# Mean over graph edges with sorted key windows: one-operand target compares, TensorE in program order, and key fetches for two slots at once

## The chip, the cores and the metric

The kernel runs on one core of one Trainium2 chip. The metric is device microseconds of one execution. A core has TensorE (PE, with its weight loads as PEld), VectorE (DVE), ScalarE (ACT), GpSimd (POOL) and SyncE (SP); each runs its own list of instructions in order, and semaphores tie the lists together.

## What is computed

One layer of a graph network: 100,000 nodes with 64 features, 3,300,000 edges sorted by target node, a self edge for every node among them.

```
h = maximum(_layernorm(x, axis=-1), 0.0)
local, nbr = h[dst], h[src]
y = concatenate([local, nbr - local], axis=-1) @ W.T + b
s, cnt = segment_sum(y, dst), segment_sum(1, dst)
x = x + where(cnt > 0, s / max(cnt, 1), 0)
```

As y is linear, each target needs only the sum of its sources' rows of h and their count. Finding and summing the source rows of 3.3 million edges is the work.

## The kernel before

`h3` holds each node's row of h as three bf16 parts (192 columns) and a column of ones. The edges go two ways.

**Gathered chunks** (`chunks`): the last 354 chunks of 3584 edges. For each group of 128 edges POOL gathers 128 rows of `h3` with an indirect DMA (L388, into `nb`, a ring of 42), DVE builds a one-hot matrix of the targets (`hot`, L331), and PE multiplies the two into `ps` (L399), 21 gathers behind the issue. After 28 of them DVE sums the three parts (L404) and POOL adds the result to `acc` in DRAM (L357, L362), due 56 gathers later.

**Windows**: the first 2.03 million edges, as 256 windows of 7936 edges. `sort_windows` sorts each window's keys by source on DVE and ACT and writes them to `ksort`; it then counts where each cell of 256 source nodes begins in each window (L596 and after) and writes these places to `at` (L627 to L636). `fill_slots` fetches for every block of 512 source nodes ("slot", 196 of them and 4 for self edges) the first 32 keys of each cell from `ksort`, 4 fetches a slot (L716, POOL, into `kf`), and makes of them source numbers (`sr_d`) and target numbers (`dt_d`, through PE transposes L740 and ACT copies L742). Keys beyond 32 in a cell are found by `find_beyond`: up to 64 per window, 128 fetches (L692 into `kx`), and then shifts on DVE (L698).

`passes` runs over 64 sets of four windows. It holds the rows of 40 slots in SBUF (`tab`, loaded at L759) and takes one step per slot and set. In a step PE picks the rows of the keys by a one-hot of the sources (L829, 4 matmuls of 128 rows, into `gp`), ACT copies them to `gs` (L831), and PE puts them to their targets by a one-hot of the targets (L838, 16 matmuls of 32 rows, into `total`). DVE makes the one-hots for 5 steps at a time, double-buffered: `gh` by one-operand compares (L808), `dh` by `one_hot`, a compare of two operands with 512 columns per step (L331). After 40 steps `total` goes to SBUF (L863, L865) and is summed (L868). The loop handles two steps, a pair, per turn.

**Stages and order.** Sort: as the sort advances, `gathers(ns)` issues one gather per 1270 ns of estimated time. Pass 0 (slots 0 to 39, 1280 pairs): `fill` and `rest` (the generators of `fill_slots` and `find_beyond`) move on every 20 pairs, after the first 16 parts of `fill` (8 groups of 5 slots) that come ahead of it; gathers go along at about 0.8 a pair, and what is left of the first 90 chunks is drained after the pass. Passes 1 to 3 are one loop body, each with 66 chunks spread evenly over its 1280 pairs; pass 4, with the self edges and the spilled keys, is two halves of 32 sets with 33 chunks each. In these halves POOL also fetches two sets of spilled rows per four windows (L794) and adds the windows' sums (L880). A scheduler orders each engine's list from the dependencies; only what `behind`, `number` or `last` name is tied to the order of the code.

## Time and profile before

| | |
|---|---|
| median of 3 runs | 17037.5 us (17037.39 to 17084.01) |
| the profiled execution, its span | 17007.46 us, 17005.8 us |
| busy: PE, DVE, ACT, POOL | 73%, 72%, 43%, 72% |
| mean granted TensorE clock | 0.838 |
| gathers `nb` | 9912, mean 1019 ns on POOL |
| `dh` compares | 12800, mean 419 ns |
| `gh` compares | 10240, mean 393 ns |
| key fetches `kf` | 784, mean 1006 ns |

A group's row reads: line, engine, operation, output and inputs, shape, count; then busy us and mean ns of one; then the engine's idle time just ahead of these instructions and what ended it. Mean durations hold the tail of an instruction, in which the next of its engine has begun; a run of the same instruction in the timeline (x5) gives their distance. A busy PE is not a PE at its peak.

### The profile page before, as it was taken

The numbers are of one execution on the slowest core, as the hardware profiler recorded it, in microseconds if no ns is written. First come the engines' busy times: TensorE is split into PE (matmuls) and PEld (weight loads), VectorE is DVE, ScalarE is ACT, GpSimd is POOL, SyncE is SP. The second block draws the span as 40 slices with busy tenths as digits, with TensorE's granted clock in tenths as the row PEclk, the third lists the DMA queues.
The fourth block names the chain that finished last, engine by engine and source line by source line (L and its number), as shares of the span: only waits on it lengthen the run. The fifth ranks groups of instructions, "written<-read, shape, count | busy, mean of one in ns | idle before, by whom it ended". The sixth has DMA issues, their size and how long they took to land. (4 is left out here: it accounts for less than half of the span.)

```text
span 17005.8 us, 639895 instructions
## 1 busy us (share of the span) xinstructions
PE 12381.4 (73%) x266812; PEld 9784.7 (58%) x266812; DVE 12270.0 (72%) x31051; ACT 7284.1 (43%) x15555; POOL 12313.7 (72%) x11723
## 2 busy tenths in 40 slices
PE   6111111559999799999699999699999698858775
PEld 5011000447777577777577777477777576647664
DVE  6999982558878687777587777587777576647663
ACT  5244480335555344444354444254444343324331
POOL 4777777665675477777677777767777778767885
PEclk7555555779999899999799999799999798879887
DMA  7322222324454455555455555455555565556556
GB/s 293 70 39 40 49 49 58 86 73 115 120 121 120 112 128 123 124 124 122 112 127 123 124 124 123 110 128 124 122 124 123 112 125 112 113 100 121 112 111 250
DMA packets 1672971, 1949.85 MB, mean 115 GB/s; under 512 B 1065318, under 2 KB 1078766, under 8 KB 1665070
## 3 DMA queue, kind: packets, MB, share of 16 engines
q1 hardware_dynamic: 1194800, 1341.60, 27.4%
q0 software_dynamic: 471200, 541.36, 20.4%
q8 instruction: 2090, 34.24, 0.8%
q10 hardware_dynamic: 4032, 25.69, 0.4%
q14 instruction: 849, 6.96, 0.1%
HBM read 1652.22 MB, written 255.28 MB: 112 GB/s over the span
## 5 line engine op out<-in xcount | busy, mean ns | idle before, releaser
L388 POOL DMA_INDIRECT nb<-h,si x9912 | 10098.9, 1019 | 3811.3 <-issue 2714.6
L831 ACT CAST gs<-gp 128x386 bf16<-128x386 f32 x12800 | 5591.9, 485 | 7358.8 <-PE gp L829 6820.4
L331 DVE TENSOR_TENSOR dh<-dt,upto 128x512 bf16<-128x512 int16 x12800 | 4575.9, 419 | 1979.7 <-PE total L838 1697.2
L838 PE MATMUL total<-gs,dh 32*128 32x193 bf16 x200704 | 5542.2, 251 | 304.8 <-DVE dh L331 288.3
L829 PE MATMUL gp<-tab,gh 128*128 128x193 bf16 x50176 | 5509.6, 253 | 129.8 <-ACT gs L831 83.6
L838 PEld LDWEIGHTS <-dh 32*128 32x128 bf16 x200704 | 4125.9, 96 | 1490.7 <-issue 1099.5
L829 PEld LDWEIGHTS <-gh 128*128 128x128 bf16 x51200 | 4404.5, 100 | 1000.1 <-issue 861.6
L399 PE MATMUL ps<-nb,hot 128*128 128x193 bf16 x9912 | 2106.6, 278 | 3659.3 <-DMA nb<-h,si 2151.3
L808 DVE TENSOR_SCALAR gh<-srs,who_f 128x768 bf16<-128x768 int16 (+1 forms) x10240 | 3415.0, 393 | 643.5 <-PE gp L829 638.5
L399 PEld LDWEIGHTS <-hot 128*128 128x128 bf16 x9912 | 896.7, 105 | 4107.8 <-issue 2294.4
L331 DVE TENSOR_TENSOR hot<-near,upto 128x512 bf16<-128x512 int16 (+1 forms) x2832 | 925.6, 382 | 397.4 <-PE ps L399 393.0
L460 ACT COPY tmp<-keys 128x1536 f32<-128x1536 f32 (+26 forms) x525 | 647.7, 1244 | 1043.3 <-DVE keys L462 880.0
L716 POOL DMA_INDIRECT kf<-ksort,at x784 | 788.5, 1006 | 238.9 <-issue 228.9
L461 DVE TENSOR_TENSOR keys<-tmp,keys 128x1536 f32<-128x1536 f32 (+26 forms) x525 | 746.8, 1457 | 68.4 <-ACT tmp L460 67.2
L462 DVE TENSOR_TENSOR keys<-tmp,keys 128x1536 f32<-128x1536 f32 (+26 forms) x525 | 748.3, 1454 | 1.1
L868 DVE TENSOR_REDUCE wsums<-whole 128x512 f32<-128x1536 f32 x320 | 613.2, 1916 | 3.7 <-issue 2.1
L404 DVE TENSOR_REDUCE sums<-ps 128x64 f32<-128x192 f32 x354 | 123.6, 349 | 535.6 <-PE ps L399 532.4
L880 POOL DMA_DIRECT2D acc<-wsums x256 | 345.1, 1348 | 105.2 <-DMA acc<-wsums 91.0
L865 DVE COPY whole<-total 128x386 f32<-128x386 f32 x640 | 325.6, 550 | 52.2 <-ACT whole L863 52.2
L536 ACT ACTIVATE junk<-keys,bound 128x543 bf16<-128x543 f32 x450 | 337.4, 750 | 16.9 <-DVE keys L462 3.6
L863 ACT COPY whole<-total 128x386 f32<-128x386 f32 x640 | 276.4, 484 | 124.8 <-PE total L838 120.8
L362 POOL DMA_DIRECT2D acc<-sums x264 | 272.7, 1033 | 42.7 <-DMA acc<-wsums 17.4
(163 smaller groups left out, 4233.2 us busy)
## 6 DMA issues: line engine op xcount, KB each, us to landing
srs<-sr_d SPq DMA_DIRECT2D x2560, 320.0 KB
nb<-h,si POOLq DMA_INDIRECT x9912
part_d<-wsums SPq DMA_DIRECT2D x256, 260.0 KB
prev<-part_d SPq DMA_DIRECT2D x256, 260.0 KB
tab<-h SPq DMA_DIRECT2D x46, 970.0 KB
dt<-dt_d SPq DMA_DIRECT2D x2560, 10.0 KB
h<-parts SPq DMA_DIRECT2D x28, 1358.0 KB
dt_d<-dt SPq DMA_DIRECT2D x40, 640.0 KB
```

Source lines behind the costliest of these rows:

```text
L331: nc.vector.tensor_tensor(out.rearrange("p k (a d) -> p k a d", d=D), numbers[:, :, None].to_broadcast(shape), upto[:shape[0], :n].rearran ...
L388: last[POOL] = nc.gpsimd.indirect_dma_start(out=nbs[e // JN][:, e % JN], out_offset=None, in_=h3, in_offset=bass.IndirectOffsetOnAxis(ap=o ...
L399: nc.tensor.matmul(ps[:, :CE], lhsT=hots_of[d // JH][:, d % JH], rhs=nbs[d // JN][:, d % JN, :CE], start=jd == 0, stop=jd == J - 1)
L460: last[ACT] = nc.scalar.copy(tmp, lo)
L461: nc.vector.tensor_tensor(lo, tmp, hi, ALU.min)
L462: last[DVE] = nc.vector.tensor_tensor(hi, tmp, hi, ALU.max)
L716: last[POOL] = nc.gpsimd.indirect_dma_start(out=kf[:, c, r * KS:r * KS + KS], out_offset=None, in_=ksort, in_offset=bass.IndirectOffsetOnA ...
L808: nc.vector.tensor_scalar(ghots[v, k][:, part, a:z].rearrange("p c i s -> p (c i s)"), srs[v, k][:, a:z].rearrange("p c i s -> p (c i s)") ...
L829: nc.tensor.matmul(gp[:, i], lhsT=ghots[v, k][:, b, c, i], rhs=of[:, :CE], start=b == 0, stop=b == NT - 1)
L831: nc.scalar.copy(gs[t], gp)
L838: nc.tensor.matmul(total[:, r, b * CE:b * CE + CE], lhsT=dh[at, i, b * P:b * P + P], rhs=rows_of[at, i, :CE], start=begin and i == 0 and b ...
L868: nc.vector.tensor_reduce(sums[:, :, :C], whole[:, :, :C3].rearrange("p k (s c) -> p k c s", s=3), axis=AX.X, op=ALU.add)
```

## The change

1. `dh` is made by `targets`: per step two compares of `upto` (256 columns) with one number per partition (f32), in place of one compare of two operands with 512 columns. `dt_d`, `dt` and `xt` hold f32 numbers, one per slot, in place of four int16 copies.
2. `in_turn` ties a PE instruction to the one that stood before it in the code: the first matmul of each pick and put and every gather matmul. The fetches of spilled keys are tied likewise on POOL.
3. A slot is now two cells that lie 196 cells apart, and cells c and c + 1 of a window follow each other in `ksort`; one fetch of 95 keys per window serves two slots (4 fetches for two, L764). DVE copies the first 32 keys to `kf`, shifts the row left by the first cell's size in six predicated copies (one per bit) and copies 32 again. `tab` is loaded in two pieces per group (16 DMAs a pass in place of 8).
4. 32 spilled keys per window are kept in place of 64: 64 fetches, four at a time, and the shift of `kx` waits four more turns and is placed behind the latest target compare. One spilled-row fetch per four windows in place of two.
5. 64 chunks per pass in place of 66; the first stage has 98 in place of 90. Additions of gathered chunks are due 14 gathers after their sums in place of 56.

```diff
-KB = 66
+KB = 64
-SPILL = 2 * KS
+SPILL = KS
+NBITS = 6
+KW = KS + 2 ** NBITS - 1
...
+        def in_turn(ins):
+            if ins.ins.engine in last:
+                tc.add_manual_dep(ins.ins, last[ins.ins.engine].ins.name,
+                                  mybir.DependencyInfo(mybir.DependencyClass.NoSync, mybir.DependencyReason.DATA),
+                                  reason="in turn")
+            last[ins.ins.engine] = ins
...
+        def targets(out, number):
+            return nc.vector.tensor_scalar(out, upto, number, None, op0=ALU.is_equal)
...
-                    nc.tensor.matmul(ps[:, :CE], lhsT=hots_of[d // JH][:, d % JH], rhs=nbs[d // JN][:, d % JN, :CE],
-                                     start=jd == 0, stop=jd == J - 1)
+                    in_turn(nc.tensor.matmul(ps[:, :CE], lhsT=hots_of[d // JH][:, d % JH],
+                                             rhs=nbs[d // JN][:, d % JN, :CE], start=jd == 0, stop=jd == J - 1))
...
-                        add_later((LAG - 1) * J, lambda q=qd, t=to0[:, u0:u0 + 1], s=sums: addition(q, t, s))
+                        add_later(JH, lambda q=qd, t=to0[:, u0:u0 + 1], s=sums: addition(q, t, s))
...
-            for w in range(P):
-                last[POOL] = nc.gpsimd.indirect_dma_start(
+            for w in range(SETS):
+                in_turn(nc.gpsimd.indirect_dma_start(
...
-                if w % 8 == 7:
+                if w % 4 == 3:
                     yield
+            for _ in range(4):
+                yield
+            xs = piece.tile([P, SETS], I32, name="xs", bufs=1)
+            with tc.issue_after(latest[0].ins):
+                nc.vector.tensor_scalar(xs, kx, 10, None, op0=ALU.logical_shift_right)
...
+                    if q < n:
+                        kw = piece.tile([P, QW, KW], I32, name="kw", bufs=3)
+                        for r in range(QW):
+                            last[POOL] = nc.gpsimd.indirect_dma_start(
+                                out=kw[:, r], out_offset=None, in_=ksort,
+                                in_offset=bass.IndirectOffsetOnAxis(ap=at[:, r, s:s + 1], axis=0))
+                        nc.vector.tensor_copy(to[0].rearrange("p (r s) -> p r s", r=QW), kw[:, :, :KS])
+                        for i in reversed(range(NBITS)):
+                            m = KS + (1 << i) - 1
+                            nc.vector.copy_predicated(kw[:, :, :m], bits[:, i, :, q:q + 1].to_broadcast([P, QW, m]),
+                                                      kw[:, :, 1 << i:m + (1 << i)])
+                        nc.vector.tensor_copy(to[1].rearrange("p (r s) -> p r s", r=QW), kw[:, :, :KS])
...
-                        one_hot(dhots[v, k][:, c], dts[v, k][:, c], CH)
+                        for i in range(2):
+                            latest[0] = targets(dhots[v, k][:, c, i], dts[v, k][:, c, i:i + 1])
...
-                    for i in range(2):
-                        last[POOL] = nc.gpsimd.indirect_dma_start(
-                            out=rows_x[:, i], out_offset=None, in_=h3,
-                            in_offset=bass.IndirectOffsetOnAxis(ap=xs[:, i:i + 1], axis=0))
+                    last[POOL] = nc.gpsimd.indirect_dma_start(
+                        out=rows_x[:, 0], out_offset=None, in_=h3,
+                        in_offset=bass.IndirectOffsetOnAxis(ap=xs, axis=0))
...
+                        if i == b == 0:
+                            in_turn(mm)
...
                 def turn(g, n, base, at, kb, final):
+                    last.pop(PE, None)
```

The instructions move in two places that matter below. On POOL, at the end of the sort, where `nb` are gathers, `acc` additions and `kf` the key fetches, before:

```order
L357 DMA acc<-sums,to 100352x65
L388 DMA nb<-h_61,si 128x194 x28
L357 DMA acc<-sums,to 100352x65
L388 DMA nb<-h_61,si 128x194 x21
L716 DMA kf<-ksort,at 128x32 x220
L388 DMA nb<-h_61,si 128x194 x7
```

and now (`kw` are the wider fetches):

```order
L372 DMA acc<-sums,to 100352x65
L403 DMA nb<-h_61,si 128x194 x28
L372 DMA acc<-sums,to 100352x65
L403 DMA nb<-h_61,si 128x194
L764 DMA kw<-ksort,at 128x95 x108
L403 DMA nb<-h_61,si 128x194 x7
L764 DMA kw<-ksort,at 128x95 x18
L403 DMA nb<-h_61,si 128x194 x7
L764 DMA kw<-ksort,at 128x95 x6
```

Counted from the start of the list, 1806 gathers stood ahead of the first key fetch, and 1589 do now; the 220 fetches that followed in a row have become 132 in three runs.

On PE, at the head of the loop body of passes 1 to 3, where `ps` are gather matmuls, `total` puts and `gp` picks, before:

```order
L838 MATMUL total<-gs,dh 128x193
L957 COMPARE_AND_BRANCH
L957 UNCONDITIONAL_BRANCH x2
L1083 BRANCH_PREFETCH_HINT
L399 LDWEIGHTS hot
L399 MATMUL ps<-nb,hot 128x193
```

and now:

```order
L414 MATMUL ps<-nb,hot 128x193
L1000 COMPARE_AND_BRANCH
L1000 UNCONDITIONAL_BRANCH x2
L1126 BRANCH_PREFETCH_HINT
L865 LDWEIGHTS gh
L865 MATMUL gp<-tab_85509,gh 128x193
```

Before, 96 gather matmuls stood ahead of the first pick of a whole pass (83 in a half pass); now the picks come first and the gather matmuls follow 1.4 to a pair. The row ahead of the branch shows the end of pass 0: before, its last puts; now 166 gather matmuls follow the last put there.

140 lines of the change are left out of this document (74 added, 66 removed).

## The prediction

> **What bounds the kernel now.** I read the page first, then groups of instructions in two stretches, then windows, waits and the timeline at the seams.
>
> ```profile
> span 17005.8 us, 639895 instructions
> PE   6111111559999799999699999699999698858775
> POOL 4777777665675477777677777767777778767885
> ```
>
> Each digit is the busy share of 425 us. The sort ends in the sixth slice, pass 0 fills 7 to 13, three whole passes 14 to 31, two half passes 32 to 39. PE looks full, yet a busy PE may be one that waits inside a pipelined stretch, so the groups decide. In the middle of pass 1 (6250 to 8000 us):
>
> ```profile
> L388 POOL DMA_INDIRECT nb<-h,si x1281 | 1312.7, 1025 | 390.2 <-issue 348.2 <-PE gp L829 23.1 <-DMA nb<-h,si 8.2
> L831 ACT CAST gs<-gp 128x386 bf16<-128x386 f32 x1776 | 775.6, 485 | 930.4 <-PE gp L829 830.7 <-PE total L838 88.6 <-ACT gs L831 6.5
> L331 DVE TENSOR_TENSOR dh<-dt,upto 128x512 bf16<-128x512 int16 x1776 | 637.1, 419 | 324.0 <-PE total L838 281.1 <-PE gp L829 37.4 <-issue 5.1
> L808 DVE TENSOR_SCALAR gh<-srs,who_f 128x768 bf16<-128x768 int16 x710 | 303.0, 427 | 44.1 <-PE gp L829 43.4
> L399 PE MATMUL ps<-nb,hot 128*128 128x193 bf16 x1287 | 270.8, 258 | 147.6 <-DMA nb<-h,si 146.6
> L808 DVE TENSOR_SCALAR gh<-srs,who_f 128x512 bf16<-128x512 int16 x710 | 255.8, 360 | 0.0
> ```
>
> POOL issues a gather every 1750/1281 = 1.366 us and waits for next to nothing but its own issue gap; PE waits for gathers (146.6 us), DVE for PE. A pair of steps (two casts) takes 1750/888 = 1.97 us, which is the 1848/1280 = 1.444 gathers of a pair times 1.366. **POOL sets the whole passes.** Pass 0 differs (3750 to 5250 us):
>
> ```profile
> L831 ACT CAST gs<-gp 128x386 bf16<-128x386 f32 x1682 | 734.2, 485 | 592.4 <-PE gp L829 565.3 <-ACT gs L831 13.8 <-PE total L838 11.5
> L388 POOL DMA_INDIRECT nb<-h,si x497 | 540.3, 1087 | 372.2 <-PE ps L399 227.1 <-issue 133.8 <-PE gp L829 6.4
> ```
>
> A pair takes 1500/841 = 1.784 us and POOL waits for PE: PE and DVE set it. Windows of 250 us, then two of 25 us (busy PE, PEld, DVE, ACT, POOL):
>
> ```profile
> 3500.00:3750.00 250.00, 81.08 (x1941) 64.22 (x1943) 68.16 (x199) 46.65 (x106) 176.65 (x182) 0.66 0.17 40
> 4250.00:4500.00 250.00, 240.54 (x5967) 192.78 (x5956) 210.71 (x593) 145.74 (x333) 152.78 (x143) 1.00 0.49 119
> 9250.00:9500.00 250.00, 228.52 (x5263) 183.18 (x5262) 194.28 (x555) 115.40 (x266) 194.31 (x190) 0.93 0.54 123
> ...
> 8275.00:8300.00 25.00, 6.43 (x20) 2.09 (x20) 1.30 (x4) 0.00 (x0) 18.98 (x20) 0.50 0.22 40
> 8475.00:8500.00 25.00, 25.00 (x640) 20.21 (x641) 21.27 (x60) 14.55 (x34) 6.57 (x7) 1.00 0.44 118
> ```
>
> The first window holds a stall, the last two a seam between passes: PE first has only gather matmuls, then runs ahead while POOL, its buffers full, issues 7 gathers where 20 fit. There a pair costs PE 25/17 = 1.47 us, about 1.55 with evacuations.
>
> **Start of pass 0.** POOL's key fetches, the first casts, and POOL's pace ahead of them:
>
> ```profile
> L716 POOL DMA_INDIRECT kf<-ksort,at x784: 940/947/2992, 2854.9 to 5386.9; - x196
> L831 ACT CAST gs<-gp x2560: 473/482/515, 3069.5 to 5597.9; 128x386 bf16<-128x386 f32 x197
> L388 POOL DMA_INDIRECT nb<-h,si x77: 940/944/1099, 2599.8 to 2699.4; - x77
> ```
>
> The new order puts 1589 gathers ahead of the first key fetch instead of 1806. At 100/77 = 1.30 us, 217 fewer are 282 us. The block of fetches shrinks from 220 to 132; at 0.947 + 0.30 us each, 88 fewer are 110 us, and PE's full pace waits for nearly all of them in both. Sum −392 us; the selection that DVE now does (22 times 2.1 us, below, ahead of the first compare, 46 us) fits beside the 100 us of the first 80 fetches, and so do the 64 scans for spilled keys that are left, which already lay there. Should DVE not keep up, the uncovered part of these 46 us comes on top.
>
> **The stall.**
>
> ```profile
> DVE xs L698 <- DMA kx<-ksort,xat: 169.1, 1, 169.1
> PE total L838 <- DVE dh L331: 166.0, 1, 166.0
> ```
>
> DVE stands before the shift of the 128 spill keys, with the one-hots that PE needs queued behind it. The window above lost about 240 − 81 = 159 us of PE. Now there are 64 fetches, four at a time, and the shift comes four turns after the last: −155 us. What is late next is PE itself, which the pace below prices. If POOL were still behind by more than those four turns (80 pairs, some 140 us), DVE would stop here again for the rest.
>
> **Pace of pass 0.** Target one-hots, from the timeline of pass 1:
>
> ```profile
> 6998.92 1.76 DVE L331 TENSOR_TENSOR dh<-dt,upto 128x512 bf16<-128x512 int16 x5
> 6999.32 2.18 POOL L388 DMA_INDIRECT nb<-h,si  x1 [0.30 <-PE gp L829]
> 7000.60 1.33 DVE L808 TENSOR_SCALAR gh<-srs,who_f 128x768 bf16<-128x768 int16 x4
> 7001.80 0.95 POOL L388 DMA_INDIRECT nb<-h,si  x1 [0.30 <-issue]
> 7004.49 1.03 POOL L388 DMA_INDIRECT nb<-h,si  x1 [0.30 <-issue]
> 7004.63 1.34 DVE L808 TENSOR_SCALAR gh<-srs,who_f 128x768 bf16<-128x768 int16 x4
> ```
>
> Five old compares take 1.76: (1.76 − 0.42)/4 = 0.335 us apart. Of the one-operand kind, four (768, 512, 768, 512 columns) take 1.33; as 256 columns more cost 427 − 360 = 67 ns, 512 come out at (1.33 − 0.36 − 0.134)/3 = 0.28 us and 256 columns at 0.21 (a line through two sizes; bounds 0.17 and the 0.28 of 512 columns). Two are 0.42 against 0.335: DVE pays 0.085 us more per step and 0.17 per pair of steps: the change makes DVE's work longer, not shorter. The selection of one pair of slots is six predicated copies of 996 elements in all and two small copies:
>
> ```profile
> L452 DVE COPY_PREDICATED s<-own,q 128x1024 int32<-128x1024 int32 (+1 forms) x16 | 20.1, 1255 | 0.4
> ```
>
> That is 1.22 us by elements, 1.7 to 2.5 with eight starts; 2.1 taken. About 65 selections remain beside 1280 pairs: 0.11 us per pair. DVE had 0.84 × 1.784 = 1.50 us of work per pair; now about 1.78 at the most, less where busy time overlaps. PE needs 1.55 plus 0.8 gather matmuls of 0.09 plus transposes, 1.68. So both engines stand near 1.7, with only two sets of one-hots between them, and neither can make up for a wait of the other. Before, 1.68 of PE's work came out at 1.784; I take 1.84 us (bounds 1.70, where nothing waits, and 2.0, where DVE's 1.78 carries the same overhead), 0.056 × 1280 = +72 us. POOL, with 1.1 issues of 1.3 us per pair, is no limit there, so the selection finds its keys landed: in program order it stands where its fetches do, and POOL can run 21 gathers ahead of that.
>
> **Drain.** 8 chunks, 224 gathers, come to this stage, whose rate of issue is unchanged; after the last step 166 gather matmuls remain. POOL is 42 buffers ahead, so 124 gathers at 1.30 are +161 us with PE idle, and 10 to the next stage (before, all gathers were issued ahead of the last steps). Pass 0 ends 392 + 155 − 72 − 171 = **304 us earlier**.
>
> **The passes.** Issue of the block tables marks each start:
>
> ```profile
> 8227.31 29.49 SPq L759 DMA_DIRECT2D tab<-h  x8
> 8257.03 4.31 SPq L770 DMA_DIRECT2D srs<-sr_d  x1
> 13461.08 29.63 SPq L759 DMA_DIRECT2D tab<-h  x8
> 15070.12 29.25 SPq L759 DMA_DIRECT2D tab<-h  x8
> L829 PE MATMUL gp<-tab,gh x1176: 243/247/369, 8352.9 to 8599.4; 128*128 128x193 bf16 x196
> ```
>
> Whole pass: (13461.1 − 8227.3)/2 = 2617 us. PE starts 126 us in, behind 96 gather matmuls; now picks come first. Tables issued in 16 pieces I cost at the same 30 us (SP only; they are one load), the source numbers follow, PE starts near +45 us, meets its first gather matmul after 15 pairs, near +70, and frees a buffer near +78. POOL has issued 42 by +55 and loses 23 us. Then 1750 gathers at 1.366 = 2390, and 17 to the next start: 2485, −132 us. The gather beside old compares took 2.18 us, those beside one-operand ones 0.95 and 1.03; for that I take 15 ns per gather (bounds 0 and 80), −26: **−158 us**, three times −474. What covers this: PE at 1.55 + 1.4 × 0.09 = 1.68 and DVE at 0.777 × 1.97 + 0.17 = 1.70 per pair stay under POOL's 1.4 × 1.35 = 1.89, so the 0.17 us that the compares add cost nothing here; without that cover they would be 0.17 × 1280 = 218 us a pass. Program order on PE costs nothing either: a stop at a gather matmul delays picks, but POOL never waits for them while its 42 buffers are free. The additions to the accumulator, due 14 gathers after their sums instead of 56, still reach POOL 33 gathers (45 us) after PE needed the last one, so I cost them at nothing.
>
> Half pass, 1609 us: POOL bounds it too, since it also adds the windows' sums and fetches spill rows without waiting (14000 to 15000 us):
>
> ```profile
> L880 POOL DMA_DIRECT2D acc<-wsums x83 | 113.3, 1365 | 1.7 <-issue 0.7 <-DMA acc<-wsums 0.7
> L794 POOL DMA_INDIRECT rows_x<-h,xs x42 | 43.3, 1030 | 12.8 <-issue 12.5 <-DMA nb<-h,si 0.3
> ```
>
> The change takes away 28 gathers × 1.366 = 38 us and one of two spill fetches per window, 32 × (1.03 + 0.30) = 43, and the 15 ns on 896 gathers, 13: −94 us, twice −188. Its seam I leave as it is (bounds −30 and +10).
>
> **Sum:** 17007.5 (span 17005.8) − 304 − 474 − 188 = 16041. The median, 17037.5, lies 30 above the profiled run: **16,070 us**.
>
> **Rivals.** (a) *The compares lock POOL out.* The place is every gather of passes 1 to 4; the price is four compares of 0.21 us per pair, 0.84 us. If POOL stood for a share f of them, 5120 pairs outside pass 0 would lose f × 0.84 × 5120 = 4300 f us, and the credit of 15 ns (105 us) goes: 20,500 at f = 1, slower than before from f = 0.2.
>
> ```profile
> L388 POOL DMA_INDIRECT nb<-h,si x189 | 180.0, 952 | 57.6 <-issue 52.1 <-PE ps L399 2.7 <-DMA nb<-h,si 2.7
> ```
>
> For it: in the sort (1000 to 1250 us), without such compares, a gather takes 952 ns, beside them 1025; all 73 ns charged to the 0.32 us of one-operand compares per gather are f = 0.23. Against: the slow gather lies beside two-operand compares. The Trainium skill, "SBUF — State Buffer", Who interferes with whom, speaks against this change: a tensor_scalar in a two-port mode blocks GpSimd fully, while tensor_tensor did not hold up descriptors. By it f would be near 1; the rows differ, 2.18 beside the latter. Chance 0.04. (b) *DVE bounds pass 0* at 2.0 us or more: +205, 16,280; 0.10. (c) *Program order gives POOL's gain back*: PE, stopping at each gather and at each set of one-hots in turn, keeps 1.97 us per pair; the whole passes stay at 2617, 16,540; for it PE's 228.5 busy of 250, against it the 1.47 us pair; 0.09. (d) Everything else 0.02. The forecast has 0.75.
>
> The predicted time is the forecast's. The range takes in (b) and the bounds of the pace of pass 0 (1280 × −0.14 = −180, +205), of the gather's length (65 ns more off 7000 gathers, −460, or none, +105) and of the start (±50), which will hardly all fall on one side: 15,780 to 16,400. A measurement can tell 0.3% (51 us) from no change; (b), (c) and the forecast all lie beyond that, so faster has 0.94, same 0.01, slower 0.05.
>
> **What would show it.** First key fetch near 2573 us, pass 0's last cast near 5120, 124 gathers after it; no wait of 100 us on kx; L831's first pick 50 us into a pass; whole passes near 2460; compares 0.21 us apart. Wrong if POOL waits for PE in mid-pass, or gathers pass 1.1 us.

## The result and the profile after

The changed kernel takes 16,590 us (median of 4 runs, 16,584.5 to 16,620.7) against 17,040.5 us for the kernel before: a ratio of 0.9734, 95% interval 0.9714 to 0.9753. The forecast was 16,070 us, with a range of 15,780 to 16,400. The profiled execution took 16,584.5 us. The sum in the prediction was 16,041 for it; the change gave 423 us of the 966 that were forecast. Eight of the experiments below fell on three chips where every whole kernel takes 1.5 times as long (25,490 to 25,889 us for the kernel before) and TensorE stands for thousands of us with no wait that the profile shows.

The groups of a stretch in the middle of pass 1, as long as the one shown before the change (5950 to 7700 us):

```profile
L403 POOL DMA_INDIRECT nb<-h,si x1230 | 1327.5, 1079 | 374.7 <-issue 324.8 <-PE gp L865 20.7 <-DMA nb<-h,si 19.8
```

POOL still sets the whole passes: its idle time is its own issue gap, and nobody holds it back. But a gather now lasts 1079 ns where it lasted 1025, and one is issued every 1750/1230 = 1.423 us instead of every 1.366. The forecast had 1.351.

Pass 0, by the groups from 3400 to 4900 us:

```profile
L403 POOL DMA_INDIRECT nb<-h,si x651 | 713.3, 1096 | 365.0 <-issue 172.2 <-PE ps L414 151.9 <-PE gp L865 16.1
...
L870 ACT CAST gs<-gp 128x386 bf16<-128x386 f32 x1620 | 704.6, 485 | 638.0 <-PE gp L865 630.2 <-ACT gs L870 3.8 <-PE total L877 1.6
```

The lines of the key fetches, the casts and the spilled keys, with the shortest, median and longest duration in ns and the first and last start:

```profile
L764 POOL DMA_INDIRECT kw<-ksort,at x392: 938/952/4672, 2567.9 to 4677.6; - x196
L870 ACT CAST gs<-gp x12800: 473/482/516, 2692.6 to 16195.8; 128x386 bf16<-128x386 f32 x197
...
L707 POOL DMA_INDIRECT kx<-ksort,xat x64: 940/949/1662, 2939.9 to 3525.8; - x64
L716 DVE TENSOR_SCALAR xs<-kx x1: 190/190/190, 3730.8 to 3730.8; 128x64 int32<-128x64 int32 x1
```

The first key fetch stands at 2567.9 us, the first cast at 2692.6 instead of 3069.5, the shift of the spilled keys 205 us behind their last fetch; no wait on `kx` is left. A pair of steps takes 1500/810 = 1.852 us.

The starts of pass 2 and of the two half passes, by the loads of the block tables on the timeline:

```profile
7847.96 32.00 SPq L794 DMA_DIRECT2D tab<-h  x16
12997.37 31.03 SPq L794 DMA_DIRECT2D tab<-h  x16
14622.72 30.20 SPq L794 DMA_DIRECT2D tab<-h  x16
```

POOL's groups in the first half pass (13500 to 14500 us):

```profile
L403 POOL DMA_INDIRECT nb<-h,si x560 | 576.3, 1029 | 170.8 <-issue 152.5 <-PE gp L865 7.6 <-DMA nb<-h,si 7.3
L922 POOL DMA_DIRECT2D acc<-wsums x80 | 104.4, 1305 | 102.8 <-DMA acc<-wsums 96.7 <-issue 6.0
```

A whole pass takes (12,997.4 − 7848.0)/2 = 2575 us (2617 before, 2460 forecast), the first half pass 1625 (1609 before, 1515 forecast). The additions' row of the kernel before, in the same stretch:

```profile
L880 POOL DMA_DIRECT2D acc<-wsums x76 | 102.7, 1351 | 28.7 <-DMA acc<-wsums 24.2 <-DMA own<-h 3.5 <-issue 0.7
```

In the half pass the gathers take about as long as before; POOL now stands 102.8 us of 1000 ahead of the window additions, and stood 28.7 there before (1.7 in the stretch that the prediction shows, 14000 to 15000 us). Over the whole execution the wait of one window addition for the landing of another has grown from 91 to 306 us.

Where the 543 us between the sum and the execution lie, by the first gather of each stage (5608.1 and 13,463.1 us before, 5292.2 and 12,998.5 now): up to pass 1 the change gave 316 us (304 forecast), in the three whole passes 149 (474), and from there to the end it cost 42 (188 forecast as gain). So −12 + 325 + 230.

The missing part of the whole passes sits in long gathers. From 5700 to 12,700 us 2.7% of the gathers lasted 1500 ns or more before, and 9.5% do now; the mean of all others went down, from 997 to 979 ns. One of the long ones on the timeline, behind a run of nine target compares:

```profile
7001.57 1.85 DVE L349 TENSOR_SCALAR dh<-upto,dt 128x256 bf16<-128x256 int16 x9
...
7003.33 1.29 DVE L342 TENSOR_TENSOR hot<-near,upto 128x512 bf16<-128x512 int16 x4
...
7003.95 1.97 POOL L403 DMA_INDIRECT nb<-h,si  x1 [0.30 <-issue]
...
7004.54 1.27 DVE L843 TENSOR_SCALAR gh<-srs,who_f 128x768 bf16<-128x768 int16 x4
```

The gather begins beside two-operand compares and ends 1.97 us later, just after a run of one-operand ones.

### The profile page after: what moved, and what is told of

It is laid out like the page before. It is cut to its first block, busy times and chain, and to the rows that moved or that the text cites. A ratio compares the mean times of both kernels' runs of the same rounds, so it can differ in the third digit from the quotient of the medians.

```text
span 16582.6 us, 651802 instructions
## 1 busy us (share of the span) xinstructions
PE 12131.2 (73%) x266300; PEld 9623.2 (58%) x266300; DVE 13165.8 (79%) x44636; ACT 7205.2 (43%) x15555; POOL 12170.2 (73%) x11203
## 5 line engine op out<-in xcount | busy, mean ns | idle before, releaser
L403 POOL DMA_INDIRECT nb<-h,si x9912 | 10419.4, 1051 | 3408.6 <-issue 2647.6
L349 DVE TENSOR_SCALAR dh<-upto,dt 128x256 bf16<-128x256 int16 x25600 | 5467.9, 301 | 1472.8 <-PE total L877 1351.0
L865 PE MATMUL gp<-tab,gh 128*128 128x193 bf16 x50176 | 5447.3, 252 | 353.0 <-DVE gh L843 206.2
L865 PEld LDWEIGHTS <-gh 128*128 128x128 bf16 x51200 | 4508.3, 99 | 1582.4 <-issue 1067.7
L877 PEld LDWEIGHTS <-dh 32*128 32x128 bf16 x200704 | 4020.7, 94 | 1469.6 <-issue 840.1
L414 PE MATMUL ps<-nb,hot 128*128 128x193 bf16 x9912 | 2247.8, 274 | 3201.4 <-DMA nb<-h,si 1696.2
L764 POOL DMA_INDIRECT kw<-ksort,at x392 | 430.4, 1098 | 233.5 <-DVE kf L767 96.3
```

The costliest lines, as they stand in the source:

```text
L349: return nc.vector.tensor_scalar(out, upto, number, None, op0=ALU.is_equal)
L403: last[POOL] = nc.gpsimd.indirect_dma_start(out=nbs[e // JN][:, e % JN], out_offset=None, in_=h3, in_offset=bass.IndirectOffsetOnAxis(ap=o ...
L414: in_turn(nc.tensor.matmul(ps[:, :CE], lhsT=hots_of[d // JH][:, d % JH], rhs=nbs[d // JN][:, d % JN, :CE], start=jd == 0, stop=jd == J - 1))
L865: mm = nc.tensor.matmul(gp[:, i], lhsT=ghots[v, k][:, b, c, i], rhs=of[:, :CE], start=b == 0, stop=b == NT - 1)
L877: mm = nc.tensor.matmul(total[:, r, b * CE:b * CE + CE], lhsT=dh[at, i, b * P:b * P + P], rhs=rows_of[at, i, :CE], start=begin and i == 0 ...
```

## The experiments

This table sums up the runs on chips where the kernel before takes 16,984 to 17,041 us. The first two, the fifth and the last are medians of four runs, the others single runs. A whole pass is half the time from the start of pass 2 to that of the first half pass; the last two columns count the gathers from 5700 to 12,700 us.

| kernel | us | whole pass | first half pass | 1500 ns or more | mean ns |
|---|---|---|---|---|---|
| before | 17,040 | 2617 | 1609 | 2.7% | 1026 |
| changed | 16,590 | 2575 | 1625 | 9.5% | 1077 |
| changed, two-operand `dh` | 16,297 | 2498 | 1608 | 2.5% | 1035 |
| before, one-operand `dh` | 17,108 | 2652 | 1608 | 7.2% | 1047 |
| changed, two-operand `dh`, POOL in written order | 16,072 | 2508 | 1495 | 2.5% | 1038 |
| changed, pauses between compares | 16,478 | 2488 | 1632 | 2.6% | 1030 |
| before, TensorE in written order | 16,503 | 2564 | 1576 | 2.5% | 1027 |
| changed, TensorE not in written order | 16,991 | 2586 | 1650 | 7.6% | 1055 |
| changed, additions due 56 gathers later | 16,235 | 2533 | 1516 | 7.8% | 1055 |
| the same, two-operand `dh` | 16,152 | 2516 | 1514 | 2.9% | 1041 |

### The compares undone, done alone, and with POOL's order: first on a chip that hid them

```diff
-                        for i in range(2):
-                            latest[0] = targets(dhots[v, k][:, c, i], dts[v, k][:, c, i:i + 1])
+                        latest[0] = one_hot(dhots[v, k][:, c], dts[v, k][:, c], CH)
```

with `dt` as four int16 copies again:

> The changed kernel with one part undone: the target one-hots dh are again made by one two-operand compare of 512 columns from int16 numbers; the program order of TensorE, the doubled key fetches and all else stay. Theory A (runs of one-operand compares on DVE hold POOL's gathers up, 76 ns per gather on the mean, all of it in gathers of 1500 ns and more): the share of such gathers falls from 9.6% to 2 to 3%, the whole passes from 2558-2576 to 2440-2480 us, the half passes from about 1617 to 1530-1560, and the kernel takes 16,050 to 16,200 us. Theory B (the compares are innocent; the passes take what they take because TensorE's order ties it to POOL): the whole passes stay within 20 us of 2570 and the kernel within 60 us of 16,585. My prediction's reading (two-operand compares are the worse neighbours): gathers grow by 15 ns, whole passes over 2590, kernel 16,680 or more.

The other way round, the one-operand compares in the kernel before, with `dt` as one f32 number per slot:

```diff
-                        one_hot(dhots[v, k][:, c], dts[v, k][:, c], CH)
+                        for i in range(2):
+                            nc.vector.tensor_scalar(dhots[v, k][:, c, i], upto, dts[v, k][:, c, i:i + 1], None, op0=ALU.is_equal)
```

> The kernel before with one part of the change done alone: dh by two one-operand compares of 256 columns from float32 numbers; no program order, no doubled fetches. Theory A: the gathers of 1500 ns and more rise from 2.2% towards 9.6%, the mean gather by 50 to 80 ns, a whole pass of 1848 gathers from 2617 to 2710-2765 us, and the kernel takes 17,450 to 17,650 us. Theory B: POOL's gathers stay at a mean of 1025 ns and a pass at 2617, 17,037 within 60 us. My prediction's reading (15 ns off each gather): whole passes near 2590, 16,900 us.

POOL's gathers and additions in written order:

```diff
-                    last[POOL] = nc.gpsimd.indirect_dma_start(
+                    in_turn(nc.gpsimd.indirect_dma_start(
...
-                    nc.gpsimd.dma_start(acc[ds(at, P)], sums, accum_op=ALU.add)
+                    in_turn(nc.gpsimd.dma_start(acc[ds(at, P)], sums, accum_op=ALU.add))
...
-                        nc.gpsimd.dma_start(acc[ds(at, CH)].rearrange("(b p) c -> p b c", p=P), of, accum_op=ALU.add)
+                        in_turn(nc.gpsimd.dma_start(acc[ds(at, CH)].rearrange("(b p) c -> p b c", p=P), of, accum_op=ALU.add))
```

> The changed kernel with one thing added: POOL's gathers and additions are held in the order in which the program is written, as TensorE's are. Theory C (the half passes lost their 100 us each because the scheduler now sets two window additions back to back in POOL's list, and the second waits for the first one's landing: 306 us of waiting, all of it before the window additions): the two additions are four gathers apart again, the wait of POOL on a window addition falls from 306 to about 90 us, the half passes from 1626 and 1608 to 1510-1540, the whole passes stay within 25 us of 2570, and the kernel takes 16,370 to 16,450 us. Rival D (the half passes are slow because their tables are loaded and their windows spilled as in any order): half passes unchanged, 16,585 within 50 us. A second rival, E: POOL held to the written order waits for PE at chunk additions, and all passes grow by 30 us or more: over 16,650 us.

And the first and the third together:

> Both edits together in the changed kernel: two-operand compares of 512 columns for dh, and POOL in written order. If theories A and C are both right and their parts add (300 us in the whole passes and 140 in the half passes from the compares, 200 in the half passes from the additions), 15,880 to 16,050 us, with whole passes of 2440-2480 and half passes of 1420-1460. If only A is right: 16,050 to 16,200. If only C is right: 16,370 to 16,450. If neither: 16,585 within 60.

Measured: 24,305, 25,429, 24,950 and 24,724 us where the kernel before took 25,521 (ratios 0.952, 0.996, 0.978, 0.969, each within 0.002). The first of them, by its page:

```profile
L403 POOL DMA_INDIRECT nb<-h,si x9912 | 9938.0, 1003 | 11187.8 <-PE ps L414 8122.6
L877 PE MATMUL total<-gs,dh 32*128 32x193 bf16 x200704 | 8075.7, 274 | 4512.7 <-issue 4257.2
```

TensorE stands 4257 us ahead of the puts for nothing that the profile shows, where the changed kernel's page has 385 us in all, and POOL waits 8123 us for TensorE. POOL bounds no pass here, so none of the expectations could be tested.

### Two-operand compares on a chip where POOL bounds the passes

> The same kernel as in the first experiment (the target one-hots by two-operand compares of 512 columns, all else as changed), run again because on the chip of that run every kernel, the one before too, took 1.5 times as long: TensorE waited there between its matmuls for nothing that the profile shows (4257 us before the sums' matmuls), so that it and not POOL set the pace of the passes, and what POOL's gathers cost could not show in the time. Where the kernel before takes about 17,040 us again: theory A expects 2 to 3% of gathers at 1500 ns or more, whole passes of 2440-2480 us, half passes of 1530-1560 and 16,050 to 16,200 us; theory B whole passes within 20 us of 2570 and 16,585 within 60 us; my prediction's reading whole passes over 2590 and 16,680 us or more.

16,297 us. The starts of pass 2 and of the half passes:

```profile
7748.62 31.41 SPq L795 DMA_DIRECT2D tab<-h  x16
12745.00 31.88 SPq L795 DMA_DIRECT2D tab<-h  x16
14353.34 30.19 SPq L795 DMA_DIRECT2D tab<-h  x16
```

The gathers' group from 5950 to 7700 us:

```profile
L403 POOL DMA_INDIRECT nb<-h,si x1276 | 1316.5, 1032 | 388.7 <-issue 338.7 <-PE gp L865 22.3 <-DMA nb<-h,si 18.9
```

The gather is back at 1032 ns, the long ones at 2.5%, a whole pass at 2498 (theory A had 2440 to 2480, and 16,050 to 16,200 us for the kernel). So the one-operand target compares cost the changed kernel 287 us: 37 up to pass 1, 214 in the whole passes, 36 after them. Theory B, that TensorE's order ties POOL down, is out, as the order was kept; so is my prediction's reading. The half passes kept their 1608: their loss has another cause.

### Gathers beside DVE work of one kind

The stages of this kernel, as lists of DVE instructions that are repeated (`two`: two-operand, 512 columns; `one` and `wide`: one-operand, 256 and 768; `tiny`: two-operand, one column):

```
[], [two], [one], [wide], [one] * 10 + [two], [one, one, tiny], [wide] * 4 + [one] * 10 + [two] * 4
```

Its first form used two buffers for DVE's results.

> POOL's gathers by themselves: it leaves out the whole computation (the output is zeros) and issues seven times 200 gathers of 128 rows of 388 bytes, beside nothing, and beside some 200 us of DVE work of one kind: two-operand compares of 512 columns, one-operand ones of 256, one-operand ones of 768, ten one-operand ones and a two-operand one in turn, two one-operand ones and a two-operand addition of one column in turn, and the mixture of a slot group (4 of 768, 10 of 256, 4 two-operand ones of 512). Theory A: alone and beside two-operand compares a gather lasts 0.95 to 1.05 us and none passes 1.5; beside unbroken one-operand compares POOL hardly gets through, and gathers last until the compares are over (tens of us or more); beside ten and one they end at the two-operand compare and last up to 2 to 4 us; with an addition after every two compares they stay under 1.5 us, if it is the unbroken run that matters. Theory B: all stages agree within 10%. My prediction's reading: beside two-operand compares gathers are longer by 15 ns or more than beside one-operand ones.

Compares of 256 columns were 0.42 us apart in the mean and 1.4 while gathers ran, since each waited for its buffer, and gathers beside them took 958 ns. Only the sixth stage came without such waits, and there gathers were long: 117 with a mean of 1398 ns, 50 of them over 1500. Its one-column additions all wrote the same column. The second form:

> The gathers by themselves again (nothing of the reference is computed, the output is zeros), with 24 buffers in turn for DVE's results, since with two of them each compare waited for the one two before it, and a 256-column compare came every 0.42 us instead of every 0.195 as in the changed kernel: there was no unbroken run in that look, and no gather beside it passed 1.2 us. Theory A: with compares back to back, gathers beside unbroken one-operand compares of 256 or 768 columns take tens of us or more, those beside ten and one end with the two-operand compare and take up to 2 to 4 us, those beside the mixture have 5 to 15% over 1.5 us, and those alone, beside two-operand compares, or beside two one-operand compares and an addition in turn have none or nearly none. Theory B: all seven stages within 10% of each other, 0.94 to 1.1 us.

POOL's gathers in five of the stages: alone, and while DVE ran two-operand compares, one-operand ones of 256 columns, of 768, and ten of 256 and a two-operand one in turn:

```profile
L108 POOL DMA_INDIRECT nb<-in_x,si x199 | 188.4, 947 | 64.2 <-issue 59.7 <-DVE si L102 3.9 <-DMA nb<-in_x,si 0.3
L108 POOL DMA_INDIRECT nb<-in_x,si x134 | 138.9, 1037 | 40.8 <-issue 40.8
L108 POOL DMA_INDIRECT nb<-in_x,si x163 | 154.0, 945 | 49.7 <-issue 49.7
L108 POOL DMA_INDIRECT nb<-in_x,si x151 | 153.5, 1016 | 46.0 <-issue 46.0
L108 POOL DMA_INDIRECT nb<-in_x,si x155 | 152.6, 984 | 47.2 <-issue 46.6 <-DVE h_one L78 0.3 <-POOL nb L107 0.3
```

The third of these on the timeline:

```profile
597.75 6.50 DVE L78 TENSOR_SCALAR h_one<-upto,who 128x256 bf16<-128x256 int16 x31
598.01 0.94 POOL L108 DMA_INDIRECT nb<-in_x,si  x1 [0.30 <-issue]
```

With compares every 0.208 us without a break, a gather takes 945 ns, as alone; beside two-operand ones it takes 1037. My theory A in this form has fallen, and the prediction's reading of the neighbours is right for pure runs. Nor does a lone two-operand compare after every ten hold gathers up: none of the 155 passed 1159 ns. Beside two one-operand compares and a one-column addition in turn, with 64 columns for the results, 158 gathers took 965 ns in the mean and none over 1030. The first form took 1398 ns beside the same instructions; it differs in the one column and in the chip, and which of the two makes it is not shown. But beside the kernel's mixture (4 of 768, 10 of 256, 4 two-operand ones) 37 of 127 gathers passed 1500 ns. The Trainium skill, "SBUF — State Buffer", Who interferes with whom, says that a `tensor_scalar` in a two-port mode shuts GpSimd out for the whole instruction and that the later of two claimants waits; the gathers beside the 256-column compares, 945 ns against 947 alone, do not show it. Whether these compares run in such a mode no run here shows.

The changed kernel says the same. Gathers from 5700 to 12,900 us that met nothing but compares on DVE, by the kinds whose times overlap theirs, in order (`gh` alternates 768 and 512 columns), counted from the trace; the expectation further down has counts that were made in another way:

```
DVE's compares under the gather        gathers   mean ns   1500 ns or more
256 columns only                          1562       965        0
768 and 512 only                           749       989        2
256, then 768 and 512                      700      1131      114
768 and 512, then 256                      270      1017       16
two-operand, then 768 and 512               97      1453       44
two-operand, then 256                      162      1287       62
256, then two-operand                       88      1019        1
```

A long gather meets more changes just because it is long, so this alone does not say which way it goes.

### Changes of form

The same kernel with other stages (runs of changing length around these numbers; `wide2`: two-operand, 768):

```
runs((two, 4), (wide, 4))
runs((one, 10), (wide, 4))
runs((two, 4), (one, 10))
runs((wide, 4), (one, 10), (two, 4))
runs((wide, 4), (one, 10), (two, 4), between=tiny)
runs((two, 4), (wide, 4), between=tiny)
runs((wide2, 4), (two, 4))
```

> Gathers by themselves beside DVE compares (nothing of the reference is computed, the output is zeros), seven stages of 200 gathers beside 270 us of runs of changing length: two-operand 512 columns and one-operand 768 in turn; one-operand 256 and 768; two-operand 512 and one-operand 256; the kernel's mixture of the three; the mixture with a two-operand addition of one column at every change of form; the first stage with that addition; and two-operand compares of 768 and 512. The look before showed gathers of 945 ns beside unbroken one-operand compares of 256 columns, as alone, so theory A's unbroken run has fallen; in that look and in the changed kernel (0 of 1088 gathers inside a 256-column run over 1500 ns, but 113 of 574 that meet a change from 256 to 768 columns, 33 of 33 that meet 768, 512 and 256) the long ones meet a change of form. Theory F (a change of DVE's form under a gather holds it up): every stage with changes between one-operand forms or from a two-operand to a one-operand one has 10 to 40% of gathers over 1500 ns, the last stage (two-operand throughout) none, and the additions at the changes do not help, being changes themselves. Theory G (only the change from two-operand to one-operand holds a gather up): the second stage has none, the first, third and fourth 10 to 40%.

POOL's gathers in the seven stages, in that order:

```profile
L130 POOL DMA_INDIRECT nb<-in_x,si x178 | 214.8, 1207 | 54.2 <-issue 54.2
L130 POOL DMA_INDIRECT nb<-in_x,si x149 | 221.8, 1489 | 45.4 <-issue 45.1 <-DVE h_one L78 0.3
L130 POOL DMA_INDIRECT nb<-in_x,si x145 | 215.9, 1489 | 44.2 <-issue 44.2
L130 POOL DMA_INDIRECT nb<-in_x,si x170 | 209.4, 1232 | 51.8 <-issue 51.8
L130 POOL DMA_INDIRECT nb<-in_x,si x173 | 209.8, 1213 | 52.7 <-issue 52.7
L130 POOL DMA_INDIRECT nb<-in_x,si x117 | 225.8, 1930 | 35.6 <-issue 35.6
L130 POOL DMA_INDIRECT nb<-in_x,si x174 | 199.0, 1144 | 53.0 <-issue 53.0
```

From the timeline of the third stage, a two-operand run between two of 256 columns, and the gather that it meets:

```profile
704.10 2.08 DVE L71 TENSOR_TENSOR h_two<-near,upto 128x512 bf16<-128x512 int16 x6
704.36 2.63 POOL L130 DMA_INDIRECT nb<-in_x,si  x1 [0.30 <-issue]
706.10 2.19 DVE L78 TENSOR_SCALAR h_one<-upto,who 128x256 bf16<-128x256 int16 x10
```

Over 1500 ns were 23 of 178 gathers, 72 of 149, 73 of 145, 36 of 170, 36 of 173, 59 of 117, and 0 of 174. The same instructions that leave gathers alone in pure runs hold them up where runs of two forms alternate, one-operand forms of 256 and 768 columns too (the second stage), so theory G is out. F holds for alternating runs, with larger shares than it gave in three stages, but not for every change: the lone two-operand compare after every ten, above, held up none. Two-operand compares throughout have no long ones, but a mean of 1144. An addition at the change itself does not help (fifth and sixth stage).

The traces also say when a long gather ends. In the third stage all 73 began in a two-operand run and none in a run of 256 columns, and they ended 0.89 to 0.90 us after the first one-operand compare that followed, however long the run before it was: the gather above ended at 706.99, and that compare began at 706.10. So here it is the two-operand run that the gather sits through, not the one-operand one. In the second stage 71 of the 72 began in a run of 768 columns.

### Pauses inside the runs

```diff
+                        tiny = pause(latest[0])
```

after every two target compares and after every source compare, `pause` being a two-operand addition of one column. Its first run was on a chip of the other kind:

> The changed kernel with a two-operand addition of one column put on DVE after every two one-operand target compares and after every source compare of 768 or 512 columns (12,800 and 10,240 more DVE instructions of some 65 to 70 ns, 1.5 ms of DVE's 3.4 idle ones). Theory A with the unbroken run as its mechanism: POOL gets through at each addition, gathers of 1500 ns and more fall from 9.6% under 2%, whole passes to 2430-2480 us although all compares are still one-operand ones; pass 0, where DVE is busiest, grows by up to 150 us; the kernel takes 16,150 to 16,400 us. If one-operand compares hold POOL up whatever stands between them: whole passes stay within 25 us of 2570 and the kernel takes 16,585 to 16,800 us. Theory B: whole passes unchanged too, 16,585 to 16,800.

24,885 us against 25,490 before, POOL waiting for TensorE; nothing follows. Then:

> The changed kernel with a two-operand addition of one column after every two one-operand target compares and after every source compare, as in the run on the disturbed chip, but with 64 places for its results in turn, so that it waits for nothing. If what holds a gather up is a one-operand instruction that DVE starts right behind another, and any break lets POOL through: gathers of 1500 ns and more under 2%, whole passes of 2430-2490 us, 16,150 to 16,400 us. Theory F (changes of form): there are more changes than before, so the share stays at 9% or rises, whole passes stay at 2560 us or more, 16,585 to 16,900 us.

16,478 us. The starts of pass 2 and of the half pass:

```profile
7916.29 31.47 SPq L811 DMA_DIRECT2D tab<-h  x16
12892.55 32.04 SPq L811 DMA_DIRECT2D tab<-h  x16
```

Whole passes of 2488 us with all one-operand compares in place: the long gathers are down to 2.6%. What it costs is pass 0, which ends 153 us later, and half passes of 1632. The passes are as the first expectation has them; the long gathers (under 2% expected) and the kernel (16,150 to 16,400) miss it by a little. Theory F as I had put it (more changes, so no fewer long gathers) fails here. The traces show which long gathers went, by the DVE instruction that was running as they began (5700 to 12,700 us):

```
long gathers, of all that began beside    hot (two-operand)   dh             gh
changed                                   126 of 293          218 of 2005    78 of 1086
changed, two-operand dh                    65 of 351           48 of 1652     0 of 1389
changed, pauses between compares          130 of 343            0 of 2210     0 of 1151
```

With the pauses no gather that begins beside a one-operand compare is held up; those that begin beside the two-operand `hot` are held up nearly as often as without. So most of the long gathers that the one-operand `dh` adds begin in one-operand runs. In the commonest kind, 110 gathers, they begin late in a run of `dh`, in the median 1.6 us after its start, and end in the median 1.39 us after the run of `gh` behind it began. What decides which gather is caught, and what in the chip does this, is not shown.

### One-operand compares in the kernel before

This is the kernel before with the one-operand compares alone, now on a chip where it takes 17,005 us.

> [...] Theory A: gathers of 1500 ns and more rise from 2.2% towards 9.6%, a whole pass of 1848 gathers from 2617 to 2700-2765 us, and the kernel takes 17,400 to 17,650 us. Theory B: a pass at 2617, 17,037 within 60 us. My prediction's reading (15 ns off each gather): passes near 2590, 16,900 us.

17,108 us. The starts of pass 2 and of the half pass:

```profile
8259.26 29.23 SPq L756 DMA_DIRECT2D tab<-h  x8
13562.56 29.27 SPq L756 DMA_DIRECT2D tab<-h  x8
```

Whole passes of 2652 us, 35 more, with 7.2% of long gathers. The direction is A's and not the prediction's, the size a third of what I expected: the same compares cost 77 us a pass in the changed kernel. Without TensorE's order the changed kernel has 7.6% and 1055 ns, with it 9.5% and 1077, so the order of the work seems to have a part in how often a gather is held up (single runs).

### POOL in written order, and the two together

> Two-operand compares for dh and POOL's list in written order, in the changed kernel. Two-operand compares alone took 16,297 us with whole passes of 2487-2496 and half passes of 1607 and 1590 (so they gave the half passes only 18 us each). Theory C (the rest of the half passes' loss is POOL's wait at the second of two window additions set back to back, 301 us in that run, against 91 us before the change): additions stand four gathers apart again, POOL's wait for a landing before them falls to about 90 us, half passes to 1480-1510, whole passes stay within 20 us of 2490, and the kernel takes 16,070 to 16,130 us. Rival D (the landing is waited for wherever the additions stand, or the half passes are bound by TensorE and DVE): half passes within 25 us of 1600, 16,260 to 16,340 us. Rival E (POOL in written order waits for the sums of PE and DVE at its additions): whole passes over 2520, 16,400 us or more.

16,072 us (median of 4; ratio 0.945, interval 0.9434 to 0.9466), the fastest version of all. The starts of pass 2 and of the half passes:

```profile
7729.39 31.50 SPq L795 DMA_DIRECT2D tab<-h  x16
12744.62 28.70 SPq L795 DMA_DIRECT2D tab<-h  x16
14239.17 27.53 SPq L795 DMA_DIRECT2D tab<-h  x16
```

The window additions from 13500 to 14500 us:

```profile
L922 POOL DMA_DIRECT2D acc<-wsums x84 | 115.1, 1370 | 8.8 <-DMA acc<-wsums 6.4 <-DVE sums L421 2.2
```

The wait ahead of the window additions is gone, and the half pass falls from 1608 to 1495 us. Theory C holds; D and E are out. POOL's list bears it out: of the 256 window additions, 30 stood directly behind another before the change, 92 do in the changed kernel, with two-operand compares too, and 6 here.

### The due time of the chunk additions

```diff
-                        add_later(JH, lambda q=qd, t=to0[:, u0:u0 + 1], s=sums: addition(q, t, s))
+                        add_later((LAG - 1) * J, lambda q=qd, t=to0[:, u0:u0 + 1], s=sums: addition(q, t, s))
```

> The changed kernel with one number undone: additions of gathered chunks due 56 gathers after their sums again, not 14. If the due time is the cause: POOL's wait for a landing ahead of the window additions falls from 306 to about 90 us or less, half passes from 1626 and 1608 to 1500-1530, whole passes within 25 us of 2570, and the kernel takes 16,360 to 16,420 us. If the single spill fetch is the cause: wait near 300, half passes within 25 us of 1617, 16,585 within 50.

16,235 us. The starts of pass 2 and of the half passes:

```profile
7829.07 31.40 SPq L794 DMA_DIRECT2D tab<-h  x16
12894.68 31.22 SPq L794 DMA_DIRECT2D tab<-h  x16
14410.31 30.13 SPq L794 DMA_DIRECT2D tab<-h  x16
```

The window additions from 13500 to 14500 us:

```profile
L922 POOL DMA_DIRECT2D acc<-wsums x88 | 119.2, 1354 | 26.4 <-DMA acc<-wsums 18.8 <-DMA acc<-sums 4.2 <-issue 3.2
```

The half pass is at 1516, and 18 window additions stand directly behind another instead of 92. One number of the change cost 247 us from the first half pass to the end. Undoing it also took 42 us off each whole pass here, where long gathers fell to 7.8%, so passes and kernel came out lower than expected; with two-operand compares it took nothing off the passes:

> The same with two-operand target compares. With the due time as the cause it should match the kernel with POOL in written order: whole passes of 2480-2500, half passes of 1460-1510, and 16,050 to 16,120 us. If POOL's written order gave more than the due time takes back: 16,120 to 16,300.

16,152 us (median of 4; ratio 0.9512, interval 0.9496 to 0.9528): whole passes of 2516, half passes of 1514. The due time does not quite match POOL's written order: the time falls in the range of the last alternative, and the written order gives some 80 us more (ratio 0.945). Why the due time changes the whole passes only beside one-operand compares is open.

### TensorE's written order

Alone in the kernel before (likewise for the first matmul of each pick and put), and taken out of the changed kernel:

```diff
-                    nc.tensor.matmul(ps[:, :CE], lhsT=hots_of[d // JH][:, d % JH], rhs=nbs[d // JN][:, d % JN, :CE],
-                                     start=jd == 0, stop=jd == J - 1)
+                    in_turn(nc.tensor.matmul(ps[:, :CE], lhsT=hots_of[d // JH][:, d % JH],
+                                             rhs=nbs[d // JN][:, d % JN, :CE], start=jd == 0, stop=jd == J - 1))
```

```diff
-            if ins.ins.engine in last:
+            if ins.ins.engine in last and ins.ins.engine != PE:
```

> The kernel before with one part of the change alone: TensorE in written order (the first matmul of each pick and put, and every gather matmul). My prediction's reading: the order alone takes out the seams of the whole passes, since picks then come ahead of the 96 gather matmuls: the first pick comes 40 to 60 us into a pass instead of 126, whole passes of 1848 gathers fall from 2617 to about 2555-2575 (132 us less 28 x 2 gathers at 1.366 us, 76 us, that only the smaller chunk count gives, is 56), and 16,750 to 16,900 us with pass 0 as before. If the order costs TensorE as much as it gives (rival c): whole passes at 2617 or more, 17,040 or more. If the order is what sets window additions back to back: POOL's idle time on a landing ahead of them rises from 91 to about 300 us and half passes stay at 1609 or grow; if not, it stays near 91.

> The changed kernel without TensorE's written order (the spilled keys' fetches keep theirs on POOL). My prediction's reading: the seams come back, whole passes from 2569 to 2610-2650 us, the first pick over 80 us into a pass. If the order is what sets the window additions back to back, POOL's wait on a landing falls from 306 to about 90 us and the half passes from 1617 to about 1520; if it is another part (additions due 14 gathers after their sums, one spill fetch between them in place of two), the wait stays near 300 and the half passes within 25 us of 1617. Gathers of 1500 ns and more stay between 6 and 10% by the account of DVE's changes of form, as all compares stay one-operand ones. Kernel: 16,550 to 16,800 us.

Both fell on a chip of the other kind (25,889 us before): 26,103 and 24,660 us. There the order alone made the kernel slower, with TensorE standing for 5653 us ahead of the puts with no wait shown. Again:

> The kernel before with TensorE in written order alone, again, for a chip on which POOL bounds the passes. My prediction's reading: the first pick comes 40 to 60 us into a pass instead of 126, whole passes of 1848 gathers fall from 2617 to 2555-2575, and the kernel takes 16,750 to 16,900 us. Rival c: whole passes at 2617 or more, 17,040 or more. If the order sets window additions back to back: POOL's idle time on a landing ahead of them rises from 91 to about 300 us and half passes stay at 1609 or grow; if not, it stays near 91.

> The changed kernel without TensorE's written order, again, for a chip on which POOL bounds the passes. My prediction's reading: the seams come back, whole passes from 2569 to 2610-2650 us. If the order sets the window additions back to back, POOL's wait on a landing falls from 306 to about 90 us and the half passes from 1617 to about 1520; otherwise the half passes stay within 25 us of 1617. Kernel: 16,550 to 16,800 us.

16,503 and 16,991 us, where the kernel before took 17,002. The starts of pass 2 and of the half pass, with the order alone:

```profile
7899.24 28.73 SPq L768 DMA_DIRECT2D tab<-h  x8
13027.93 29.12 SPq L768 DMA_DIRECT2D tab<-h  x8
```

The same of the changed kernel without it:

```profile
8201.29 31.94 SPq L794 DMA_DIRECT2D tab<-h  x16
13372.73 30.10 SPq L794 DMA_DIRECT2D tab<-h  x16
```

Its window additions over the whole execution:

```profile
L922 POOL DMA_DIRECT2D acc<-wsums x256 | 337.0, 1316 | 387.1 <-DMA acc<-wsums 345.2 <-issue 37.5 <-DMA acc<-sums 4.3
```

The order alone brings whole passes of 2564 us, in the middle of the 2555 to 2575 expected. The kernel is faster than the expected 16,750 to 16,900 us, because pass 1 also starts 260 us earlier (first gather at 5348.2): with the order alone 1589 gathers stand ahead of the first key fetch, as in the changed kernel; the changed kernel without the order has 1805. So it is TensorE's order that brings the first fetch forward. All the rest of the change gives nothing that can be told from noise without the order (16,991 us, 11 less; 16,550 to 16,800 expected). Passes fell back to 2586, less than the 2610 to 2650 expected, and the first pick again came 125 us after the first load of the pass's tables. POOL's wait stays at 345 us, so the order does not set the window additions back to back; half passes, at 1650, are longer than the expectation had them.

## Why the prediction was wrong

**Right, and for the reasons given.** POOL bounds the passes before and after. Pass 0 as a whole: pass 1 starts 316 us earlier (304 forecast), with the first key fetch at 2567.9 (near 2573 forecast), no stall on `kx`, 1.852 us a pair (1.84), compares 0.196 us apart (nine in 1.85 us on the timeline, the last one's 0.28 taken off, over 8; forecast 0.21), and 132 gathers after the last cast (124). The seam: the first pick comes 39.5 us after the first load of the pass's tables (7887.5 and 7848.0; "50 us into a pass"), and the order alone is worth 53 us of a pass beside the 76 of 56 gathers fewer. Rival (b) did not come, nor (c): at 2575 the passes are 42 us shorter, and that (c)'s 16,540 us lies near the measured time is chance.

**The start of pass 0, part by part.** The prediction derived 392 us from fewer gathers ahead of the key fetches (282) and fewer fetches (110); the first cast came 377 us earlier. The runs say where the gathers' part comes from: with TensorE's order alone the first key fetch stands at 2568.6 instead of 2854.9, 286 us earlier. Without the order the rest of the change starts pass 1 at 5606.3, 2 us earlier than before, where the prediction's other terms of pass 0 (110 + 155 − 72 − 171) add up to 22.

**Wrong, first step: the gather's length.** "For that I take 15 ns per gather (bounds 0 and 80)": a gather beside one-operand compares should be shorter. The ordinary ones are, by 18 ns (997 to 979) and in the pure runs by 92. But the mean rose by 51 ns, because 9.5% instead of 2.7% are held up. I read the evidence for the step wrongly: the gather of 2.18 us that I laid to two-operand compares began beside them at 6999.32 and ended at 7001.50, inside the one-operand run that began at 7000.60. It met a change of form and ended 0.90 us after it, just as the long ones of the third stage above. The bounds, 0 and 80 ns shorter, left out the side on which it fell. With two-operand compares the passes take 2498, near the forecast's 2485 without the credit. Undoing the compares gives 287 us. Why one-operand compares leave more gathers to be held up stays open.

**Rival (a)** had the neighbour right, with the sign that I gave 0.04, and the mechanism wrong: one-operand compares do not lock POOL out. In its terms the 250 us from pass 1 on are f = 250/4300 = 0.06, below the 0.2 from which it was slower. (Its 0.32 us of one-operand compares per gather come to 0.35 by the rows, 710 × (0.28 + 0.35) over 1281, which makes its f of 0.23 a 0.21.)

**Wrong, second step: the additions.** "The additions to the accumulator, due 14 gathers after their sums instead of 56, still reach POOL 33 gathers (45 us) after PE needed the last one, so I cost them at nothing." That was an argument on the chunk additions alone. The window additions stand in the same list of things due; with the chunk additions at 14, the scheduler set 92 of them directly behind another in POOL's list instead of 30, and 38 with one instruction between instead of 6, and the second stands there until the first has landed (126 such waits, 306 us; 32 waits and 91 us before). I had quoted the very row (1.7 us of waiting in 1000) and did not ask what kept it so small. Undoing the number gives 247 us from the first half pass on, the whole of the 230 missing there. That the shared list is the way from the one to the other is argued from the code, not shown; that the due time alone does it, and that POOL's written order also undoes it, is shown.

With both steps undone the kernel takes 16,072 to 16,152 us, near the forecast of 16,070. In part that is luck: in the profiled execution of the faster version the three whole passes take 112 us more than the sum has for them, while pass 0 ends 50 us sooner and what follows the whole passes takes 36 us less.

## What to carry to other kernels

Judge a neighbour on another engine by what it does at the changes between kinds of instruction, and look at the share of long instructions beside the mean: here ordinary gathers became shorter while the mean grew. When a change alters one due time in a shared list, look at everything that stands in that list. Undo the parts one at a time: of this change one part, TensorE's order, gave 500 us alone, and two others together took about 430 us back (16,590 against 16,152 with both undone).

## What the runs showed of the hardware

- A gather of 128 rows takes 947 ns alone, 945 beside an unbroken run of one-operand compares of 256 columns, 1016 beside those of 768, 1037 beside two-operand ones, and 1207 to 1930 where runs of two or three of these forms alternate on DVE. It takes 984 where a lone two-operand compare stands after every ten one-operand ones, and 1144 where two-operand compares of 768 and 512 columns alternate.
- In runs of two-operand and 256-column compares in turn, a gather begun in the two-operand run ended 0.89 to 0.90 us after the next one-operand compare began (73 of 73 over 1500 ns).
- Short two-operand additions inside the one-operand runs, written to 64 columns in turn, bring the long gathers from 9.5% to 2.6% in the kernel; at the changes alone they do not help, and where all wrote one column, on another chip, 50 of 117 gathers passed 1500 ns.
- Of two window additions with at most one instruction between them in POOL's list, the second waited 2.4 us in the mean for the first one's landing (306 us in 126 waits).
- On three of the chips every whole kernel took about 1.5 times as long (the kernel before 25,490 to 25,889 us instead of 16,984 to 17,041). TensorE stood there for 3721 to 5653 us ahead of the puts with no wait that the profile shows, and it was busy for longer too: with two-operand compares 15,966 us, against 12,034 for the same kernel elsewhere, at a mean granted clock of 0.755 against 0.879. What the cause is, and whether the clock is part of it, is not shown. Which part of a kernel pays was different there: TensorE's written order alone made it slower (26,103 against 25,889).
